# One of seven block products in the first adjacency product of a four-layer GNN is split into seven once more, and layer 0's node weights are loaded later

## The chip, the cores and the metric

The kernel runs on one core of one Trainium2 chip as a single launch. The metric is the device time of an execution in microseconds (us). Engine names are those of the profile: PE is TensorE's matmul and PEld its weight load, DVE is VectorE, ACT is ScalarE, POOL is GpSimd, SP is SyncE, which here only issues DMAs.

## The reference

`x` is 8 batches x 2048 nodes x 64 features, `adj` is a dense 2048 x 2048 matrix, and all is float32. Four layers follow each other, each `x = layernorm(x + f(x))`:

```
layer 0: f = sum over k of (A_k x) w_k(node) + bias(node)
         A_0 = I, A_1 = adj, A_2 = 2 adj adj - I
         w_k(node) = sum over d of embedding[node, d] * weight[d, k]     (d = 16)
layer 1: twice  z = relu(adj z W_i)
layer 2: x W_self + adj x W_neigh + bias
layer 3: [x, adj x, 2 adj adj x - x, and the last two again] W + bias
```

So the kernel has seven products of `adj` with a 2048 x 512 matrix (8 batches x 64 features side by side). The first of them, `adj x`, is the one that the change touches; the second, `adj (adj x)`, also belongs to layer 0 and uses the node weights.

## The kernel before

**Products by seven.** Each product except the first is cut by Winograd's form of Strassen's scheme: `adj` and the right factor are cut into 2 x 2 blocks, and seven block products of sums of blocks replace eight. The function `product` does this twice: its seven outer products are named A11, S1, A12, S2, S4, S3, A22, in this order, and the helper `inner` cuts each of them again into seven (the calls `mul`, four 128x512 matmuls each in layer 0). The sums of `adj`'s blocks that all later products need are made once, during the first product, and written to DRAM in the tensors `comb`.

**The first product, by slices.** `adj` arrives in four row slices of 512 rows, each in four chunks of 1 MB (`slice_chunk`, L157, on SP's queue, into a ring of four buffers). Slice 0 is computed plainly (`plain_slice`, L792). Slices 1 to 3 (`fast_slice`) use one level of the seven products: each is 16 matmuls 128x256 (`mul`, L829), 8 for each half of the columns. `raw(I, J)` is a block of the slice itself, `summed(S1)` and the like are sums of blocks that DVE makes in `prepare` (L643), tiles `si` and `so`. POOL's queue writes these to `comb` (L655). `T[0]` to `T[3]` are the four sums of blocks of x, so that `t_of(4)` stands for the fourth. The product of the slice's last quarter with it is `pd = mul(bank(), raw(1, 1), t_of(4))`, at L856; DVE later adds it to `p1` as `u3` (L851).

A slice's result `hT` is stored to DRAM (`keep_t1`, L771, SP's queue) and turned back into node order by `back`: four transposes on PE (L457) into a PSUM tile `pt` of the pool `p_tn`, which has two banks, and a copy by ACT (L458). A list of such jobs, `pump`, is served by one step after each half of a `mul`.

**Node weights of layer 0.** The tile `wn` holds weight[:, k] for three k, on both halves of the partitions. `load_weights`, after slice 0, loads it by two DMAs of 768 KB on SP's queue (L592), ahead of the small weights. In slice 2, `sum_wn` combines the three parts on DVE and subtracts the mean over the output features (`center`, L585 and L586). `wn` is first read by the matmuls of `feature0` (L970), in the second product.

**From the first product into the second.** The pools of the first product are closed and their memory is given to the pool `l0y`: `e_sb` (the embedding, loaded on POOL's queue, L938), `xT`, `tT` and `s`. `fetch` (L952) loads `xT` from the input and `tT` from the stored first product, on SP's queue. The `a` tiles of the second product come one for each `mul` from `blocks` (L203) or `comb` (L205), 1 MB each, in the ring of four, also on SP's queue. `product` takes an argument `between`, a function that is called after the outer products A11 and S1; the second product had none.

**Order.** A scheduler sets the order of the instructions on each engine and queue from the data dependencies; only instructions under `tc.keep_in_program_order` keep the order of the code among themselves. Each engine and each queue then runs in that order.

Of the kernel before, what the change touches and what calls it, by code (L numbers as in the profile page):

```python
# [9 lines left out]
F32 = mybir.dt.float32  # L10
AF = mybir.ActivationFunctionType
ALU = mybir.AluOpType
# [4 lines left out]
P = 128  # L17
EPS = 1e-5
GW = 512
TG = GW // P  # L20
# [83 lines left out]
def kernel(  # L104
# [358 lines left out]
    class Norm:  # L463
# [111 lines left out]


    if True:
        l0 = first.enter_context(tc.tile_pool(name="l0", bufs=1))

        wn = l0.tile([P, 3, D, F], F32, tag="wn", name="wn")  # L580

        def center(w, half=slice(0, P), pin=lambda inst: inst):
            shape = list(w.shape)
            m = small.tile([P, shape[1]], F32, tag="wm", name="wm")[half]
# [3 lines left out]
            ))  # L588

        def load_weights():  # L590
            for k in range(2):
                nc.sync.dma_start(wn[k * F : (k + 1) * F], w_l0.rearrange("n i d o -> i n d o"))  # L592
            nc.gpsimd.memset(wd, 0.0)
            w3 = sums.tile([P, 5, F], F32, tag="t", name="w3", bufs=5)
            for k in range(2):
                half = slice(k * F, (k + 1) * F)
                for i, src in ((W1A, w_l1[0]), (W1B, w_l1[1]), (W2N, w_neigh), (W2S, w_self)):
                    nc.sync.dma_start(wd[half, i, half], src)
                nc.scalar.dma_start(w3[half], w_l3.rearrange("(k i) o -> i k o", i=F))
            nc.sync.dma_start(b2, b_l2.to_broadcast([P, F]))  # L600
            nc.sync.dma_start(b3, b_l3.to_broadcast([P, F]))
            return w3

        def sum_wn():
            pin = tc.keep_in_program_order
            pin(nc.vector.tensor_tensor(wn[:, 0], wn[:, 0], wn[:, 2], ALU.subtract))
            pin(nc.vector.tensor_scalar(wn[:, 2], wn[:, 2], 2.0, None, ALU.mult))
            center(wn.rearrange("p n d o -> p (n d) o"), pin=pin)

        def sum_weights(w3):  # L610
            pin = tc.keep_in_program_order
# [26 lines left out]
        def prepare(ns, ch, outers):  # L638

            ch = [c.rearrange("p m i n -> p i m n") for c in ch]  # L640

            def add(out, a, b, op=ALU.add):
                inst = nc.vector.tensor_tensor(out, a, b, op)  # L643
                if ns:

                    tc.keep_in_program_order(inst)

            def kept(tag, shape, bufs):
                s = sums.tile([P, *shape, GW], F32, tag=tag, name="s" + ("i" if tag == "C" else "o"), bufs=bufs)
                n = "ab"[: len(shape)]  # L650
                return s, s.rearrange(f"p {' '.join(n)} (m n) -> p {' '.join(n)} m n", m=TG)

            def keep(q, s0, src):
                dst = comb[q][s0 : s0 + src.shape[1]].rearrange("s p (n c) -> p s n c", n=TG)
                nc.gpsimd.dma_start(dst[:, :, ns], src)  # L655

            def inner(q, q00, q01, q10, q11):
                flat, s = kept("C", (4,), 4)
                add(s[:, 0], q10, q11)
                add(s[:, 1], s[:, 0], q00, ALU.subtract)  # L660
                add(s[:, 2], q00, q10, ALU.subtract)
                add(s[:, 3], q01, s[:, 1], ALU.subtract)
                keep(q, 4, flat)

            def raw(I, J):
# [12 lines left out]
            def sq(s):  # L678
                return lambda c: s[:, :, c].rearrange("p a (m n) -> p a m n", m=TG)

            def put(q, s):
                flat = s.rearrange("p a b c -> p (a b) c")
                keep(q, 0, flat[:, :2])
                keep(q, 3, flat[:, 3:])
                inner(q, *(flat[:, k].rearrange("p (m n) -> p m n", m=TG) for k in range(4)))


            inner(A12, *raw(0, 1))
            inner(A22, *raw(1, 1))
# [12 lines left out]
            put(S4, s4)  # L702
            yield

        with tc.tile_pool(name="p_n", bufs=4, space=PSUM) as p_n, tc.tile_pool(
# [61 lines left out]
            def bank():  # L767
                return p_n.tile([P, GW], F32, tag="mm", name="ps_n")
# [7 lines left out]
            def new_h():  # L776
                return sums.tile([P, GW], F32, tag="t", name="hT", bufs=5)

            def back(ns, p, hT):
                to_nodes(1, p_tn, slice(ns, NT, TG), p, hT)  # L780
                yield
# [25 lines left out]
            def fast_slice(ns, ch, held):  # L807
# [5 lines left out]
                def raw(I, J):  # L813
                    return lambda j, m: ch[2 * J + j][:, m, 2 * I : 2 * I + 2]
# [7 lines left out]
                def t_of(n):  # L822
                    return lambda k, p: T[n - 1][:, k // 2, k % 2, ts(p, 2 * F)]

                def mul(ps, a, b, start=True):

                    for p in range(2):
                        for k in range(NT // 2):
                            nc.tensor.matmul(  # L829
                                ps[:, ts(p, GW // 2)], b(k, p), a(k // TG, k % TG),  # L830
                                start=(start and p == k == 0), stop=(k == NT // 2 - 1),
                                skip_group_check=True,
                            )
                        pump.step()
                    return ps
# [13 lines left out]
                def plus(tag, a, b):  # L849
                    u = sums.tile([P, GW], F32, tag=tag, name=tag)  # L850
                    nc.vector.tensor_tensor(u, a, b, ALU.add)  # L851
                    return u

                next(parts)
                p2 = mul(bank(), raw(0, 1), x_of(1, 0))
                pd = mul(bank(), raw(1, 1), t_of(4))  # L856
                load_chunks(ns + 1, 2, 3)
                for job in held:
                    pump.add(back(*job))
# [1 line left out]
                pa = mul(bank(), raw(0, 0), x_of(0, 0))  # L861
                p1 = sums.tile([P, GW], F32, tag="p1", name="p1")
                nc.scalar.copy(p1, pa)
                q3 = plus("u3", pd, p1)
                done(0, p2, p1)
                if ns == TG - 1:
                    join_bias(0, 1)
# [3 lines left out]
                load_chunks(ns + 1, 0, 1)  # L871
                if ns == 1:
                    sum_weights(w3)
                elif ns == 2:
                    sum_wn()
                else:
                    join_bias(0, 0)
                pb_ = mul(bank(), summed(S2), t_of(2))
                u2 = plus("u2", pb_, p1)
# [13 lines left out]
            for ns in range(TG):  # L893
                ch = [chunks.pop((ns, j)) for j in range(NG)]
                if ns == 0:
                    for n, _ in enumerate(prepare(ns, ch, {})):
                        if n == 1:
                            sums_of_x()
                    hT = plain_slice(ns, ch)
                    w3 = load_weights()  # L900
                    load_chunks(1, *AHEAD)
                    pump.add(biases())
                else:
                    hT = fast_slice(ns, ch, held)
                for p in range(NP):
                    keep_t1(ns, p, hT[p])

                held = []
                for p in range(NP):
                    if ns == TG - 2:  # L910
                        held.append((ns, p, hT[p]))
                    else:
                        pump.add(back(ns, p, hT[p]))
# [20 lines left out]
        if True:  # L934
            p_y = first.enter_context(tc.tile_pool(name="p_y", bufs=3, space=PSUM))
            l0y = first.enter_context(tc.tile_pool(name="l0y", bufs=1))
            e_sb = l0y.tile([P, NT, D], F32, tag="e_sb", name="e_sb")
            nc.gpsimd.dma_start(e_sb, emb)  # L938


            order = [
# [51 lines left out]


            RUNS = {S2: NP, S3: NP}
            product(1, then(feature0, 0, gap=4, pool_sq=True), rate=4, runs=RUNS)


    late = p_z = None
# [127 lines left out]
```

## Time and profile before

| what | value |
|---|---|
| median of 3 runs | 1670.58 us (1670.14 to 1670.74) |
| profiled execution | 1670.91 us, span of its instructions 1669.1 us |
| granted TensorE clock | 1.00 throughout |
| PE busy | 1660.6 us of 1669.1 |
| DVE, ACT, POOL busy | 945.8, 265.3, 246.0 us |
| slice 0 of the first product | PE from 5.7 to 61.0 us |
| slices 1, 2, 3 | PE from 61.0, 113.65, 163.75 to 213.9 us |
| second product begins | 216.2 us |
| first matmul with `wn` | about 312 us |

All times in the text count from the start of the span. A matmul of float32 stands in the trace as two records, so "x16" in a row of 128x256 matmuls is eight instructions; the time from the start of one record to that of the next is its pace, which is shorter than its duration since they overlap. The profile's bracket `[0.34 <-ACT xy L458]` says how long the engine stood idle before a row and what ended that. In rows of queues (SPq, POOLq) the time is that of issuing; the landing of a transfer is given apart.

### The profile page before, as it was taken

The page shows a single profiled execution, that of the slowest core. Times are in us where ns is not written, and L with a number is a line of the kernel's source. Part 1 is how long each engine was busy: PE and PEld are TensorE (multiplying, and loading weights), DVE is VectorE, ACT ScalarE, POOL GpSimd, SP SyncE. Part 2 cuts the span into 40 slices and gives each one's busy share as a digit, 9 for nine tenths or more (in the row PEclk, how much of TensorE's full clock was granted, in tenths as well). Part 3 has the DMA queues.
Part 4 walks back from the last instruction along what each step waited for, and adds up shares of the span by engine and source line. Part 5 has one row for each costly group of instructions (what it writes and reads, how often), then busy time and mean ns, then how long its engine had stood idle before and what let it go on. Part 6 is the DMA issues. An engine that isn't in the chain of part 4 may idle for free.

```text
span 1669.1 us, 20686 instructions
## 1 busy us (share of the span) xinstructions
PE 1660.6 (99%) x8182; PEld 1046.5 (63%) x8182; DVE 945.8 (57%) x1695; ACT 265.3 (16%) x766; POOL 246.0 (15%) x332
## 2 busy tenths in 40 slices
PE   9999999999999999999999999999999999999998
PEld 4688854444444444444454455589998455579998
DVE  6497884556456456654434365873568344443657
ACT  0100000142143044430010011220001011100001
POOL 1121200254155056650000000000000000000000
PEclk9999999999999999999999999999999999999999
DMA  9898898504603700019877877667888866678884
GB/s 352 331 373 310 302 334 307 189 27 147 227 26 108 271 26 26 26 51 369 286 264 272 308 263 253 229 225 260 297 297 295 306 212 232 229 267 292 316 308 171
DMA packets 82431, 391.52 MB, mean 235 GB/s; under 512 B 8896, under 2 KB 25536, under 8 KB 42784
## 3 DMA queue, kind: packets, MB, share of 16 engines
q1 hardware_dynamic: 69520, 346.78, 58.8%
q0 software_dynamic: 11248, 42.08, 6.6%
q10 hardware_dynamic: 1568, 1.35, 0.3%
q8 instruction: 65, 1.06, 0.3%
q14 instruction: 30, 0.25, 0.0%
HBM read 339.85 MB, written 50.33 MB: 234 GB/s over the span
## 4 chain that ended last, share of the span: by engine, by line
PE 98%; DMA 1%; DVE 0%; ACT 0%; issue 0%; ACTq 0%; DVEq 0%
PE y L970 20%; PE mmb L272 17%; PE mma L272 12%; PE mmc L272 12%; PE mmb L265 9%; PE ps_n L829 8%; PE mma L265 6%; PE mmc L265 6%; PE ps_n L792 3%; PE z L1022 3%; PE z L1051 2%; DMA a<-in_slices 1%; PE pt L1013 1%; DMA xy<-in_x 0%; PE pt_n L457 0%; PE mmd L265 0%
## 5 line engine op out<-in xcount | busy, mean ns | idle before, releaser
L272 PE MATMUL mmb<-a,t 128*128 128x512 f32 x648 | 292.0, 593 | 0.0
L980 DVE SCALAR_TENSOR_TENSOR xy<-y,e_sb,xy 128x128 f32<-128x128 f32 x512 | 179.6, 351 | 141.2 <-PE y L970 125.3
L272 PEld LDWEIGHTS mmb<-a,t 128*128 128x128 f32 x648 | 121.5, 190 | 145.3 <-issue 143.5
L989 POOL TENSOR_TENSOR s<-s 128x512 f32<-128x512 f32 (+2 forms) x192 | 157.1, 818 | 333.4 <-ACT s L984 323.2
L984 ACT ACTIVATE s<-y,e_sb 128x128 f32<-128x128 f32 x512 | 139.0, 382 | 231.8 <-PE y L970 231.8
L223 DVE TENSOR_TENSOR u<-mmb,p 128x512 f32<-128x512 f32 x84 | 57.8, 689 | 181.8 <-PE mmb L272 126.0
L265 PE MATMUL mmb<-t,a 128*128 128x128 f32 x1344 | 156.9, 275 | 0.0
L265 PEld LDWEIGHTS mmb<-t,a 128*128 128x128 f32 x1344 | 153.4, 192 | 0.0
L970 PE MATMUL y<-wn,xT 64*128 64x512 f32 x512 | 131.5, 590 | 0.0
L970 PE MATMUL y<-wn,tT 64*128 64x512 f32 x512 | 131.2, 589 | 0.0
L970 PE MATMUL y<-wn,C 64*128 64x512 f32 x512 | 131.2, 589 | 0.0
L272 PE MATMUL mma<-a,T 128*128 128x512 f32 x256 | 115.5, 594 | 0.0
L272 PE MATMUL mmc<-a,t 128*128 128x512 f32 x216 | 97.3, 592 | 0.0
L287 ACT COPY p<-mma 128x512 f32<-128x512 f32 x42 | 24.6, 586 | 404.4 <-PE mma L272 262.9
L970 PEld LDWEIGHTS y<-wn,xT 64*128 64x128 f32 x512 | 49.3, 187 | 61.2 <-issue 60.7
L970 PEld LDWEIGHTS y<-wn,tT 64*128 64x128 f32 x512 | 49.6, 187 | 60.3 <-issue 60.3
L970 PEld LDWEIGHTS y<-wn,C 64*128 64x128 f32 x512 | 49.6, 187 | 60.3 <-issue 60.3
L272 PE MATMUL mma<-a,xy 128*128 128x512 f32 x192 | 86.7, 593 | 0.0
L272 PEld LDWEIGHTS mma<-a,T 128*128 128x128 f32 x256 | 47.6, 190 | 56.8 <-issue 56.5
L223 DVE TENSOR_TENSOR C<-mmc,C 128x512 f32<-128x512 f32 x48 | 33.2, 692 | 85.9 <-PE mmc L272 75.1
L272 PEld LDWEIGHTS mmc<-a,t 128*128 128x128 f32 x216 | 40.0, 190 | 45.4 <-issue 45.2
L829 PE MATMUL ps_n<-a,xy 128*128 128x256 f32 x288 | 64.7, 380 | 0.1
(140 smaller groups left out, 2047.2 us busy)
## 6 DMA issues: line engine op xcount, KB each, us to landing
a<-comb SPq DMA_DIRECT2D x240, 1024.0 KB, 4.8
a<-in_blocks SPq DMA_DIRECT2D x54, 1024.0 KB, 4.8
comb<-si POOLq DMA_DIRECT2D x28, 1024.0 KB, 10.5
a<-in_slices SPq DMA_DIRECT2D x15, 1024.0 KB, 9.4
comb<-so POOLq DMA_DIRECT2D x16, 512.0 KB, 6.7
comb<-so POOLq DMA_DIRECT2D x16, 256.0 KB, 8.4
t1T<-hT SPq DMA_DIRECT2D x16, 256.0 KB, 4.2
xT<-in_xT SPq DMA_DIRECT2D x16, 256.0 KB, 3.4
```

The source lines that it names most:

```text
L223: nc.vector.tensor_tensor(out, a, b, op)
L265: nc.tensor.matmul(to, a[:, k, m, :], xb[:, m, :], start=(start and opens and m == 0), stop=(m == TG - 1), skip_group_check=True,)
L272: nc.tensor.matmul(ps, xb[:, m, :], a[:, :, m, :], start=(start and m == 0), stop=(m == TG - 1), skip_group_check=True,)
L287: nc.scalar.copy(p1, pa)
L792: mm = nc.tensor.matmul(ps[p], xcol(0, TG * j + m, p), ch[j][:, m], start=(n == 0 and m == 0), stop=(n == NG - 1 and m == TG - 1), skip_gr ...
L829: nc.tensor.matmul(ps[:, ts(p, GW // 2)], b(k, p), a(k // TG, k % TG), start=(start and p == k == 0), stop=(k == NT // 2 - 1), skip_group_ ...
L970: mm = nc.tensor.matmul(y[:, b, :], terms[n][half, ts(k, P)], wn[half, n, h * DH : (h + 1) * DH, :], start=(n == 0), stop=(n == 2),)
L980: nc.vector.scalar_tensor_tensor(acc, y[:, :, ts(d, F)], e, acc, ALU.mult, ALU.add)
L984: nc.scalar.activation(s[:, d], y[:, :, ts(d, F)], AF.Copy, scale=e)
L989: nc.gpsimd.tensor_tensor(s[:, :n], s[:, :n], s[:, n : 2 * n], ALU.add)
L1022: nc.tensor.matmul(z[:, k, :], aT[:, ts(k, P)], wd[:, w, :], start=(n == 0), stop=(n == len(terms) - 1),)
L1051: nc.tensor.matmul(z[n][:, k], xT[half, ts(k, P)], w[half], start=True, stop=True)
```

## The change

1. In slices 1 to 3, the product `raw(1, 1)` times `t_of(4)` is no longer 16 matmuls 128x256 but a second level of seven products (`two_level`), each four matmuls 128x128: 28 matmuls. They go in turn to two banks of the pool `p_tn`, that of the transposes, and ACT copies each result out before the bank is used again. DVE joins the parts by two additions and adds `p1`.
2. The sums of `adj` that the second level needs are the `si` tile of A22 that DVE made already; it is now made ahead of that of A12. The sums of x, tile `t4`, are made once in slice 0 by four more DVE additions 128x512 (`sums_t`).
3. The pool `l0` is gone. `wn` is now a tile of `l0y`, in memory of the first product, and its two DMAs of 768 KB are on POOL's queue, after `e_sb`. `sum_wn` is the `between` of the second product, and centers the three parts one by one.

```diff
-        wn = l0.tile([P, 3, D, F], F32, tag="wn", name="wn")
...
         def load_weights():
-            for k in range(2):
-                nc.sync.dma_start(wn[k * F : (k + 1) * F], w_l0.rearrange("n i d o -> i n d o"))
...
+            outers[A22] = inner(A22, *raw(1, 1))
             inner(A12, *raw(0, 1))
-            inner(A22, *raw(1, 1))
...
+            def sums_t(b, t):
+                b11, b12, b21, b22 = b
+                for n, (x, y) in enumerate(((b12, b11), (b22, t[0]), (b22, b12), (b21, t[1]))):
+                    nc.vector.tensor_tensor(t[n], x, y, ALU.subtract)
+
+            b4 = [T[3][:, 2 * j : 2 * j + 2, :, ts(p, 2 * F)] for j in range(2) for p in range(2)]
+            t4 = xs.tile([P, 4, TG, 2 * F], F32, tag="t4", name="t4")
+            t4 = [by_tiles(t4[:, n]) for n in range(4)]
+            turn = [0]
+
+            def two_level(raw, sums_, b, t, out):
+                banks = [p_tn.tile([P, TG, P], F32, tag="pt", name="ps_i")[:, 0] for _ in range(2)]
+                pa, pb_ = banks[:: 1 - 2 * (turn[0] % 2)]
+                turn[0] += 1
...
+                part = xs.tile([P, 3, P], F32, tag="part", name="part", bufs=2)
+
+                def mul(ps, n, x, start, to):
+                    for m in range(TG):
+                        nc.tensor.matmul(
+                            ps, x[:, m // 2, m % 2], s[n](m), start=(start and m == 0),
+                            stop=(m == TG - 1), skip_group_check=True,
+                        )
+                    nc.scalar.copy(to, ps)
+
+                mul(pa, 0, b11, True, part[:, 0])
+                mul(pb_, 5, t2, True, part[:, 1])
+                mul(pa, 1, b21, False, out[:, 0, 0])
+                mul(pb_, 6, t3, False, part[:, 2])
+                mul(pa, 4, t1, True, out[:, 1, 1])
+                mul(pb_, 3, t4, False, out[:, 0, 1])
+                mul(pa, 7, b22, False, out[:, 1, 0])
+                o = out.rearrange("p a b n -> p (a b) n")
+                nc.vector.tensor_tensor(
+                    o[:, 1:], o[:, 1:], part[:, 0].unsqueeze(1).to_broadcast([P, 3, P]), ALU.add
+                )
+                nc.vector.tensor_tensor(o[:, 2:], o[:, 2:], part[:, 1:], ALU.add)
...
                 p2 = mul(bank(), raw(0, 1), x_of(1, 0))
-                pd = mul(bank(), raw(1, 1), t_of(4))
+                q3 = new_out("u3")
+                two_level(
+                    lambda i, j: lambda m: ch[2 + j][:, m, 2 + i], outers[A22], b4, t4, by_blocks(q3)
+                )
                 load_chunks(ns + 1, 2, 3)
...
-                q3 = plus("u3", pd, p1)
+                nc.vector.tensor_tensor(q3, q3, p1, ALU.add)
...
-                elif ns == 2:
-                    sum_wn()
-                else:
+                elif ns == TG - 1:
                     join_bias(0, 0)
...
             nc.gpsimd.dma_start(e_sb, emb)
+            wn = l0y.tile([P, 3, D, F], F32, tag="wn", name="wn")
+            for k in range(2):
+                nc.gpsimd.dma_start(wn[k * F : (k + 1) * F], w_l0.rearrange("n i d o -> i n d o"))
+
+            def sum_wn():
+                pin = tc.keep_in_program_order
+                pin(nc.vector.tensor_tensor(wn[:, 0], wn[:, 0], wn[:, 2], ALU.subtract))
+                pin(nc.vector.tensor_scalar(wn[:, 2], wn[:, 2], 2.0, None, ALU.mult))
+                for n in range(3):
+                    center(wn[:, n], pin=pin)
...
-            product(1, then(feature0, 0, gap=4, pool_sq=True), rate=4, runs=RUNS)
+            product(1, then(feature0, 0, gap=4, pool_sq=True), sum_wn, rate=4, runs=RUNS)
```

More of the change, by code (lines that the diff above doesn't have):

```diff
@@ L577 @@
     if True:
-        l0 = first.enter_context(tc.tile_pool(name="l0", bufs=1))
-        wn = l0.tile([P, 3, D, F], F32, tag="wn", name="wn")
         def center(w, half=slice(0, P), pin=lambda inst: inst):
@@ L602, in load_weights @@
             return w3
[L604 to L608, printed above, removed]
         def sum_weights(w3):
@@ L663, in inner @@
                 keep(q, 4, flat)
+                return flat
             def raw(I, J):
@@ L777, in new_h, with by_tiles @@
                 return sums.tile([P, GW], F32, tag="t", name="hT", bufs=5)
+            def by_tiles(v):
+                return v.rearrange("p (a b) c -> p a b c", b=2)
+            def sums_t(b, t):
[3 more added lines that the diff above has]
+            b4 = [T[3][:, 2 * j : 2 * j + 2, :, ts(p, 2 * F)] for j in range(2) for p in range(2)]
@@ new lines @@
+            t4 = xs.tile([P, 4, TG, 2 * F], F32, tag="t4", name="t4")
[5 more added lines that the diff above has]
+                turn[0] += 1
+                b11, b12, b21, b22 = b
+                t1, t2, t3, t4 = t
+                s = [raw(i, j) for i in range(2) for j in range(2)]
+                s += [lambda m, n=n: sums_[:, n, ts(m, P)] for n in range(4)]
+                part = xs.tile([P, 3, P], F32, tag="part", name="part", bufs=2)
[18 more added lines that the diff above has]
+                nc.vector.tensor_tensor(o[:, 2:], o[:, 2:], part[:, 1:], ALU.add)
@@ L779, in back, with new_out, by_blocks @@
+            def new_out(tag):
+                return sums.tile([P, GW], F32, tag=tag, name=tag)
+            def by_blocks(v):
+                return v.rearrange("p (a b n) -> p a b n", a=2, b=2)
             def back(ns, p, hT):
@@ L895 @@
                 if ns == 0:
-                    for n, _ in enumerate(prepare(ns, ch, {})):
+                    outers = {}
+                    for n, _ in enumerate(prepare(ns, ch, outers)):
                         if n == 1:
                             sums_of_x()
+                            sums_t(b4, t4)
                     hT = plain_slice(ns, ch)
```

## The prediction

> **What bounds the kernel now.** I read the page first (busy shares, then the chain that ended last), then PE's timeline over the first product, the chain over the same stretch, and the issues of SP's queue where the second product begins. Busy shares and chain, from the page:
>
> ```profile
> PE 1660.6 (99%) x8182; PEld 1046.5 (63%) x8182; DVE 945.8 (57%) x1695; ACT 265.3 (16%) x766; POOL 246.0 (15%) x332
> ...
> PE 98%; DMA 1%; DVE 0%; ACT 0%; issue 0%; ACTq 0%; DVEq 0%
> ```
>
> PE is idle for 8.5 us in all and is 98% of the chain. So PE time that is taken away is gained, and a wait of PE that is added is lost, unless it falls into one of those few gaps. The price of a matmul is its pace. PE's timeline: first three rows of 128x256 records in the slices, then two of 128x128 records with the same 128x128 weights in a later product (start, duration, records).
>
> ```profile
> 78.29 4.00 PE L829 MATMUL ps_n<-a,xy 128*128 128x256 f32 x16
> ...
> 136.13 13.98 PE L829 MATMUL ps_n<-so,T 128*128 128x256 f32 x64
> 149.94 13.98 PE L829 MATMUL ps_n<-so,xy 128*128 128x256 f32 x64
> ...
> 1102.58 3.74 PE L265 MATMUL mmb<-t,a 128*128 128x128 f32 x32
> 1106.15 3.74 PE L265 MATMUL mma<-xy,a 128*128 128x128 f32 x32
> ```
>
> Start to start, 64 records of 256 columns take 13.81 us, 215.8 ns each; 32 of 128 columns take 3.57 us, 111.6 ns each. The first row is 0.38 us longer than its like (3.62). The chain of waits over the first 330 us shows why:
>
> ```profile
> 61.23 19.03 DMA a<-in_slices
> 80.30 1.99 PE ps_n L829 x8
> ```
>
> Slice 1's last chunk of adj is issued at 61.23 and lands at 80.26; PE waits for it. Elsewhere in the slices PE has no gap. The second place is the start of the second product. SP's issues there, and PE's row that reads the last of them:
>
> ```profile
> 214.51 2.65 SPq L771 DMA_DIRECT2D t1T<-hT  x4
> 219.23 1.11 SPq L952 DMA_DIRECT2D tT<-t1T  x2
> 220.43 0.38 SPq L205 DMA_DIRECT2D a<-comb  x1
> ...
> 230.32 3.60 PE L272 MATMUL mmc<-a,C 128*128 128x512 f32 x8
> ```
>
> SP stores slice 3's result, waits until that has landed, loads it back (tT), and only then issues the `a` tile of the fifth inner product. It lands 7.7 us later, at 228.15; PE begins its weights at 229.89. **1.7 us is all the margin there.** Two of the windows of 5 us around it (busy times by engine, clock, DMA share, GB/s) show the DMA engines full:
>
> ```profile
> 210.00:215.00 5.00, 4.92 (x26) 4.04 (x25) 1.12 (x4) 0.00 (x0) 0.00 (x0) 1.00 1.00 406
> 215.00:220.00 5.00, 4.66 (x18) 2.48 (x19) 4.96 (x7) 2.25 (x4) 0.00 (x0) 1.00 1.08 378
> ```
>
> **What the skill says.** (a) The Trainium skill, "DMA: Bandwidth & Descriptors", section "Issuing engines are not separate DMA queues": DMAs of all issuing engines end on the same 16 DMA engines and interleave. The trace agrees: between 210 and 220 us SP's queue holds 54% of them and POOL's 50%, at 392 GB/s together. Moving `wn` to POOL's queue therefore gives it no bandwidth of its own. (b) "TensorE: Matmul & The Clock Gate", section "LDWEIGHTS (loading the stationary operand)": 128 columns of weights take P/1.2, 107 ns. A 128-column record needs one such load, and the trace's pace of 111.6 ns lies just above it; halving the columns gives 52% of the time, not less. (c) "ScalarE: Activation LUTs", section "What ACT_TABLE_LOAD costs": 186 ns + 0.833 ns an element without pointer operands. That makes 613 ns for 512 elements, against 586 measured (L458), so I take 293 ns for ACT's new 128x128 copies, an estimate.
>
> **The change, part by part.**
>
> *1. The product itself.* Removed in each of three slices: 16 matmuls, 32 records x 215.8 ns = 6.91 us. Added: 28 matmuls, 56 records x 111.6 = 6.25 us. Gain 0.66 us a slice, 1.97 in all. An eighth of the multiplications is saved, and of that the weight loads leave three quarters.
>
> *2. Turns between the two banks.* Each group of four matmuls takes 0.893 us, and its bank is written again one group later. Transposes show the turnaround: the copy by ACT starts 0.04 us after the last record's end and PE goes on 0.06 us after the copy. From the next group's start: 0.16 (the last record's overlap) + 0.04 + 0.29 + 0.06 = 0.56 us, below 0.893, and below 0.65 too, when PE would like to begin the weights. Cost 0; what hides it is the group on the other bank. The transposes before share the banks, but the reversed order on every second slice puts the bank used last second. If the estimate is too low by up to 0.3 us, five or six turns in three slices lose up to 0.2 us each, so 0 to 3 us; below nothing is excluded, since no wait is taken away here.
>
> *3. DVE in the slices.* Added per slice: two joins (by columns at 685 ns per 512, 0.5 and 0.4 us), and four sums of x once (2.7 us). DVE waits 6.9 us in slice 0 for a write to `comb`, and 7.3 in slice 2 and 6.0 in slice 3 for `p1`; these cover them. The first sums of A22 are made 2.4 us earlier than now, in slice 2 by 118 us against 121 us when PE needs them. `sum_wn` leaves slice 2, 8.6 us of DVE that PE did not wait for. Cost and gain 0.
>
> *4. The chunk of slice 1.* PE arrives 0.66 us earlier at a transfer that lands at 80.26. If it lands as now, slice 1 gains nothing. If it lands over 1 us earlier, the 0.38 us wait goes as well: gain 1.04. For earlier: `wn` (1.57 MB, about 4 us at 392 GB/s) leaves the queue ahead of it. Against: `wn` had landed by 37 us, and the issue at 61.23 follows PE's last use of the buffer, which does not move. I take half, 0.5, with 0 and 1.04 as ends. Slices 2 and 3 give 1.31.
>
> *5. The load of `wn`, moved.* In the order that the scheduler gives POOL, the first half stands after `e_sb` (200.5 us now, released by PE's last use of the closed pool), then two writes of sums to `comb` (205.1 and 207.6), then the second half. All of 1.57 MB is put on DMA engines that are full from 208 on: 3.8 to 4.0 us of work. The stores of slice 3 (512-byte rows) come behind or between, so tT is issued later, and behind it on SP the `a` tile of the fifth inner product. Delay of that tile: 4 us, less what fits in holes between 200 and 206 (about 1 us). Minus the margin of 1.7 us: **a new wait of PE of about 1.3 us**, ends 0 and 2.2. The next tiles have margins of 3 and 4 us and, being delayed no further, cost nothing more. The two `comb` writes behind the first half are not read before the outer products S4 and S3, over 60 us on.
>
> *6. `sum_wn` in the second product.* Now 1.22 + 0.69 + 3.35 + 3.35 us; in three parts 1.22 + 0.69 + 3 x (1.2 + 1.2) = 9.1 us, an estimate from the same rows. In DVE's order it is spread between S1's last addition (264.9 us) and A12's evictions. Added up in that order, `u` is ready at 273.0 with its bank wanted at 274.95, the next at 276.7 against 278.4, the third at 280.3 against 281.8. Margins of 1.5 us or more: cost 0. Its input landed some 40 us earlier.
>
> **Sum:** -1.31 - 0.5 + 0 + 1.3 = -0.5 us against the profiled execution's 1670.91, so 1670.4; the median of the runs lies 0.33 below that execution, so **1670.1 us**. After 290 us the order on every engine is the same as before.
>
> **Rivals.**
>
> *A. The new DMA wait takes most of the gain (the forecast).* For: the full DMA engines and the margin of 1.7 us. Against: the stretch's first 6 us aren't full. -1.3 to +0.9 us, by the ends of the wait: 1669.3 to 1671.5. Chance 0.52.
>
> *B. No new wait.* The delayed stores shift by less than 1.7 us because the second half of `wn` finds holes. Then -1.8 us, with the whole of part 4 -2.35: 1668.8 to 1668.2. Chance 0.33. To pass 0.2% (3.3 us) it would also need a gain that I can't name; I give that 0.08 of the 0.33.
>
> *C. The turns between the banks decide, and it is slower.* If a turn takes longer than 0.893 us, PE waits at every one of 15 turns. Against a gain of 1.8 us it becomes slower from 0.12 us a turn, that is from a turnaround of 1.01 us; with the DMA wait from 0.03 us. It passes 0.2% with 0.26 us a turn, 1.15 us in all. Against: a copy four times as wide turned in 0.85. With 0.26 us a turn and the DMA wait the result is 1674. Chance of C 0.15, about half of it beyond 0.2%.
>
> That the change doesn't do what it says is no rival: PE's order in the changed program shows the 28 matmuls in three slices.
>
> **How the numbers follow.** About 0.2% is what a measurement of this kernel can tell from no change; that is 3.3 us, from 1667.2 to 1673.9, and both likely cases lie inside. Faster by more: 0.08. Within: 0.85 (A 0.52, B 0.25, half of C 0.08). Slower: 0.07. The range takes B's best, 1668.2, and A with slice 1's gain lost and the wait at its upper end, +0.9 and some tenths of C: 1671.9.
>
> **What would show each step.** Right: 56 records of `ps_i` in about 6.25 us without a gap, a wait of PE on a DMA of `a` at the fifth inner product near 228 us, no wait of PE on DVE near 265 to 280. Wrong: gaps on ACT between groups of `ps_i` (part 2); no wait near 228 and a second product that begins and goes on 2 us earlier (part 5); the chunk of slice 1 landing at 80.3 again (part 4); PE waiting for `u` on DVE (part 6). A result outside 1668 to 1672 would mean a cost or gain that is not in this list.

## The result, and the profile after

The changed kernel takes **1676.39 us** (median of 6 runs, 1675.31 to 1677.32) against 1670.61 for the kernel before (6 runs on the same chip, 1670.14 to 1670.91): a ratio of 1.0035, with a 95% interval of 1.0022 to 1.0047. It is 5.8 us slower. The forecast was 1670.1, between 1668.2 and 1671.9. The profiled execution took 1676.53 us, 0.14 above the median (before: 0.30 above); its span is 1674.6.

Busy shares and the chain of the page, after:

```profile
PE 1661.0 (99%) x8254; PEld 1049.6 (63%) x8254; DVE 951.6 (57%) x1709; ACT 270.5 (16%) x787; POOL 246.8 (15%) x334
...
PE 98%; DMA 1%; DVE 0%; issue 0%; SPq 0%; DVEq 0%
```

PE is still the bound, and its busy time has grown by 0.4 us although multiplications were taken away. Two places explain all of it. The first is what was meant. PE's timeline in slice 1 (start, duration, records) begins and ends the second level so:

```profile
70.42 1.06 PE L798 MATMUL ps_i<-a,xy 128*128 128x128 f32 x8
...
75.82 1.06 PE L798 MATMUL ps_i<-si,xy 128*128 128x128 f32 x8
76.72 3.62 PE L873 MATMUL ps_n<-a,xy 128*128 128x256 f32 x16
```

From 70.42 to 76.72 the 56 records take 6.30 us, without a gap; slices 2 and 3 take 6.30 and 6.25. The row after them, which had waited 0.38 us for a chunk, no longer waits: the chunk lands at 75.98 us. The second product begins at 213.80 us; it began at 216.15. **Up to there the change has gained 2.35 us**: 1.88 in the three products, 0.38 at the chunk, and 0.09 that was there already at the start of slice 1 (60.95 us instead of 61.04).

The second place is the fifth inner product of A11. PE's timeline there:

```profile
213.80 1.02 PE L272 MATMUL mma<-a,xy 128*128 128x512 f32 x2
...
224.54 3.60 PE L272 MATMUL mmb<-a,C 128*128 128x512 f32 x8
233.82 5.85 PE L272 MATMUL mmc<-a,C 128*128 128x512 f32 x8 [5.68 <-DMA a<-comb]
239.51 3.60 PE L272 MATMUL mmb<-a,C 128*128 128x512 f32 x8
```

Two things stand in the third row. In brackets: PE was idle for **5.68 us** until the `a` tile had landed. And the eight records took 5.85 us instead of 3.60; from this start to the next are 5.69 us, where the pace gives 3.43, so **some 2.3 us more**. Four windows of 2 us (busy times by engine, then granted clock, DMA share, GB/s) show why:

```profile
230.00:232.00 2.00, 0.00 (x0) 0.00 (x0) 2.00 (x3) 0.00 (x0) 0.00 (x0) 0.85 0.97 398
232.00:234.00 2.00, 0.18 (x1) 0.21 (x2) 1.87 (x1) 0.00 (x0) 0.00 (x0) 0.50 1.06 446
...
236.00:238.00 2.00, 2.00 (x3) 0.67 (x2) 0.00 (x0) 0.00 (x0) 0.00 (x0) 0.50 1.06 446
238.00:240.00 2.00, 2.00 (x6) 0.83 (x5) 0.29 (x1) 0.00 (x0) 0.00 (x0) 0.94 0.82 348
```

The clock falls to half at about 231.4 us, 3.3 us after PE became idle at 228.14, and is back at about 238.2. The sum -2.35 + 5.68 + 2.3 = +5.6 us is the difference between the two profiled executions (1676.53 - 1670.91 = 5.62). So nothing else of size has to be looked for.

Why the tile came late stands in the rows of SP's queue:

```profile
212.17 8.10 SPq L760 DMA_DIRECT2D t1T<-hT  x4
225.06 0.81 SPq L1010 DMA_DIRECT2D tT<-t1T  x2
225.96 0.38 SPq L205 DMA_DIRECT2D a<-comb  x1
```

The four stores of `t1T` take SP 8.10 us to issue instead of 2.65, and the first lands at 224.99, 12.8 us after its issue (4.7 before). tT waits for it, and the `a` tile stands behind tT: issued at 225.96 and landed at 233.68, though PE came for it at about 228. The second half of `wn` landed at 224.79, just ahead of that first store. The windows of 5 us, with the last number the GB/s moved:

```profile
205.00:210.00 5.00, 5.00 (x24) 4.40 (x24) 2.84 (x3) 0.00 (x0) 1.37 (x2) 1.00 1.01 267
210.00:215.00 5.00, 4.58 (x26) 3.21 (x25) 3.28 (x5) 1.66 (x3) 0.00 (x0) 1.00 1.00 340
```

The DMA engines are full (share 1.01 and 1.00) and yet move only 267 and 340 GB/s; before, the same two windows had 388 and 406. **Full engines with fewer bytes: the load of `wn` costs more than its bytes.** That became the last question of the study.

### The profile page after: what moved, and what is told of

It reads as the page before. It is cut to its first block, busy times and chain, and to the rows that moved or that the text cites. A ratio compares the mean times of both kernels' runs of the same rounds, so it can differ in the third digit from the quotient of the medians.

```text
span 1674.6 us, 20882 instructions
## 1 busy us (share of the span) xinstructions
PE 1661.0 (99%) x8254; PEld 1049.6 (63%) x8254; DVE 951.6 (57%) x1709; ACT 270.5 (16%) x787; POOL 246.8 (15%) x334
## 3 DMA queue, kind: packets, MB, share of 16 engines
q10 hardware_dynamic: 1568, 1.35, 0.3%
q8 instruction: 66, 1.08, 0.3%
## 4 chain that ended last, share of the span: by engine, by line
PE 98%; DMA 1%; DVE 0%; issue 0%; SPq 0%; DVEq 0%
PE y L1028 20%; PE mmb L272 17%; PE mmc L272 12%; PE mma L272 11%; PE mmb L265 9%; PE ps_n L873 7%; PE mma L265 6%; PE mmc L265 6%; PE ps_n L836 3%; PE z L1080 3%; PE z L1109 2%; PE ps_i L798 1%; PE pt L1071 1%; DMA t1T<-hT 1%; DMA a<-comb 0%; PE pt_n L457 0%
## 5 line engine op out<-in xcount | busy, mean ns | idle before, releaser
L1080 PEld LDWEIGHTS z<-wd,C 128*128 128x128 f32 x384 | 50.2, 192 | 21.7 <-issue 20.7
```

The costliest lines, as they stand in the source:

```text
L1080: nc.tensor.matmul(z[:, k, :], aT[:, ts(k, P)], wd[:, w, :], start=(n == 0), stop=(n == len(terms) - 1),)
```

## The experiments

Theory L: the whole loss is the load of `wn` at the end of the first product, which delays the stores of `t1T`, through them tT, and on SP's queue the `a` tile; the half clock follows from PE's idle time. Rival P: the product by seven, or the sums that moved with it, costs something of its own. Rivals within L: SP's order against plain bandwidth, and the size of the load. Each kernel was timed beside the kernel before, on the same chip; the median of the kernel before was 1670.5 to 1670.7 us each time.

Slice 1 begins between 60.4 and 61.4 us in the twelve traces. To compare executions that start a little apart, the table counts from the second product's first matmul. PE comes to the fifth inner product 14.2 us after it if nothing holds it up, and loads the weights, the `a` tile, 0.4 us earlier.

| kernel | median, us | ratio to before (95% interval) | `a` tile lands after, us | wait of PE, us |
|---|---|---|---|---|
| before | 1670.6 | | 12.0 | 0 |
| changed | 1676.39 | 1.0035 (1.0022 to 1.0047) | 19.9 | 5.68 |
| no load | 1668.40 | 0.9988 (0.9981 to 0.9995) | 12.1 | 0 |
| move only | 1678.21 | 1.0048 (1.0031 to 1.0065) | 19.8 | 5.59 |
| tT on POOL's queue | 1670.14 | 0.9998 (0.9989 to 1.0007) | 15.1 | 0.86 |
| load late | 1668.56 | 0.9989 (0.9982 to 0.9995) | 12.2 | 0 |
| second half late | 1672.04 | 1.0009 (1.0002 to 1.0016) | 16.2 | 1.94 |
| two queues | 1676.50 | 1.0036 (1.0023 to 1.0049) | 20.4 | 6.23 |
| six pieces | 1675.06 | 1.0030 (1.0019 to 1.0042) | 19.0 | 4.76 |
| all partitions | 1672.13 | 1.0008 (0.9999 to 1.0017) | 16.0 | 1.84 |
| four matmuls more | 1674.32 | 1.0027 (1.0017 to 1.0036) | 19.6 | 1.89 |
| two matmuls more | 1675.82 | 1.0032 (1.0020 to 1.0045) | 19.9 | 3.91 |

Three of these kernels have a wait of about 1.9 us in their profiled execution (second half late, all partitions, four matmuls more). Part of their runs (12 of 20, 8 of 12 and 4 of 10) are longer, most of them by about 2 us, and list a mean clock of 0.997 or 0.998 instead of 0.999 or 1.000, which lifts the medians. In those the clock seems to have fallen; no trace of one was taken, and the part on the half clock comes back to it.

### No load, and the move alone

```diff
-            for k in range(2):
-                nc.gpsimd.dma_start(wn[k * F : (k + 1) * F], w_l0.rearrange("n i d o -> i n d o"))
+            nc.gpsimd.memset(wn, 0.01)
```

> The changed kernel with one thing left out: the two transfers of wn. POOL fills the tile with a constant instead, so the node features of layer 0 are not those of the reference; every other instruction stays. Theory L (the whole loss comes from the load at the end of the first product): the second product begins at 213.8 us as in the changed kernel, the stores of t1T land 4 to 5 us after their issue (12.8 in the changed kernel), the wait of 5.68 us before the fifth inner product is 0 to 0.6 us, the granted clock stays 1.00, and the time is 1670.6 - 2.35 = 1668.2 us, up to 1668.8. Theory P (the product by seven, its sums on DVE or the weight sums in the second product cost something that the trace hides): some 1670 us or more, with a wait that is still there without the load.

Measured: 1668.40 us. The second product begins at 213.53, the stores of `t1T` land 5.4 to 5.6 us after their issue (a little over the expected 4 to 5), and the fifth product follows without a wait; the clock is 1.00 in every window from 205 to 275 us. SP's queue and the row of PE:

```profile
211.90 2.60 SPq L760 DMA_DIRECT2D t1T<-hT  x4
217.33 1.05 SPq L1009 DMA_DIRECT2D tT<-t1T  x2
218.47 0.38 SPq L205 DMA_DIRECT2D a<-comb  x1
```

```profile
227.71 3.60 PE L272 MATMUL mmc<-a,C 128*128 128x512 f32 x8
```

The second experiment is the other half, the kernel before with only the load and `sum_wn` moved:

```diff
-        wn = l0.tile([P, 3, D, F], F32, tag="wn", name="wn")
...
+            wn = l0y.tile([P, 3, D, F], F32, tag="wn", name="wn")
+            for k in range(2):
+                nc.gpsimd.dma_start(wn[k * F : (k + 1) * F], w_l0.rearrange("n i d o -> i n d o"))
```

> The kernel before, with the moved load of wn and its moved sums alone; the fourth quarter stays one plain product. Theory L: the second product begins at 216.15 us as before, the load makes the a tile of the fifth inner product land at about 233.7 us as in the changed kernel, where it is needed at 229.9: a wait of 3.8 us, and if that idle time also halves the clock another 2.4 us: 1674.4 us without and 1676.8 us with the clock. Theory P: the load costs nothing by itself, 1670.6 us.

Measured: 1678.21 us, above both numbers. PE's timeline:

```profile
226.83 3.60 PE L272 MATMUL mmb<-a,C 128*128 128x512 f32 x8
236.02 5.17 PE L272 MATMUL mmc<-a,C 128*128 128x512 f32 x8 [5.59 <-DMA a<-comb]
```

The wait is 5.59 us, not 3.8. My expectation had kept the landing time of the changed kernel, 233.7 us, but POOL's second half of `wn` follows the last writes to `comb`, and those follow the slice: everything behind it moves with the end of the first product (landing at 235.89). This kernel also shows where the 0.38 us at the chunk of slice 1 come from: here, too, the chunk lands early, at 77.10 us, and PE's row, at 78.62, takes 3.62 us and has no wait, though the product is the plain one. So that gain belongs to the load, which is no longer ahead of the small weights, and not to the product by seven. In the trace 5.59 + 1.6 for the half clock - 0.4 at the chunk is 6.8 us; the profiled executions differ by 7.04 and the medians by 7.56.

So theory L holds and P falls. The kernel without the load is 2.3 us faster than the one before (1668.40), of which, by the traces, 1.9 are the product by seven and 0.4 the chunk. The moved load costs 7.6 us alone, with the 0.4 already taken off; 7.6 - 1.9 is 5.7, and the result was 5.8.

### SP's order, or bandwidth

Here only the first two loads of tT leave SP's queue for POOL's:

```diff
-                        nc.sync.dma_start(tile_, src[p][:, ts(i, GW)])
+                        queue = nc.gpsimd if src is t1T and k < 2 else nc.sync
+                        queue.dma_start(tile_, src[p][:, ts(i, GW)])
```

> The changed kernel with the first two loads of tT on POOL's queue, behind wn, so that SP's queue does not wait for the stores of t1T before it issues the a tiles; the same bytes are moved in the same stretch. Theory Q (the loss is SP's order: the a tile was issued at 226 us because tT stood ahead of it): the a tile is issued at 215 to 219 us, lands before 228, the wait is 0 to 0.5 us, 1668.2 to 1668.8 us. Theory B (the loss is bandwidth: the 16 DMA engines are busy from 198 to 235 us, and the same bytes need the same time whatever their order): the eighth a tile still lands near 240 us where it is needed at 237.9, the waits of PE come to 2 to 4 us in smaller pieces, each too short for the clock to fall: 1670.5 to 1672.5 us.

Measured: 1670.14 us, 1.7 above the kernel without the load: between the two theories. SP's queue and PE:

```profile
212.62 7.83 SPq L760 DMA_DIRECT2D t1T<-hT  x4
220.54 0.72 SPq L205 DMA_DIRECT2D a<-comb  x1
```

```profile
229.46 3.67 PE L272 MATMUL mmc<-a,C 128*128 128x512 f32 x8 [0.86 <-DMA a<-comb]
```

The stores still land at 225.08, 12.5 us after their issue, but nothing on SP waits for them now. The tile is issued at 220.54 instead of 225.96, and the wait shrinks from 5.68 to 0.86 us, too little for the half clock. **So most of the loss is the wait in SP's order behind tT, and only the rest can be bandwidth.** The 7.83 us of the first row show what remains: SP is still held up while it issues the stores. The later tiles came some 0.1 us late each (the fifth and sixth products take 3.5 us from start to start); the two to four microseconds that theory B saw there did not come. The wait and these come to 1.0 of the 1.7 us; in the two traces the other 0.7 lies in the start of slice 1, at 61.40 instead of 60.67 us.

### The load later

Each half now waits for a result of the second product, by a one-column copy on ACT:

```diff
+                for k, late in enumerate((u[:, 1], v[:, 0])):
+                    half = slice(k * F, (k + 1) * F)
+                    nc.scalar.copy(wn[half, 0, 0, :1], late[half, :1])
+                    nc.gpsimd.dma_start(wn[half], w_l0.rearrange("n i d o -> i n d o"))
+                sum_wn()
```

> The changed kernel with the two halves of wn loaded later: ACT writes one column of each half from a result of the second product (the seventh inner product of A11, the third of S1), and POOL's transfer of that half follows it, so the halves start near 238 and 248 us; the order on PE, DVE and SP is that of the changed kernel. Theory L: the stores of t1T and the a tile of the fifth inner product come as in a kernel without the load, and the 1.5 MB go into the gaps of the DMA engines between 238 and 271 us (share 0.75 to 0.93 there), where four a tiles are on the way at a time: 1668.2 to 1668.8 us. Rival: the load costs the same wherever it lies beside the a tiles, since each half slows them by some 4 us and two tiles on the way have only about 1.4 us of margin each: waits of 2 to 5 us, 1670.5 to 1673 us.

Measured: 1668.56 us, a ratio of 0.9989 (0.9982 to 0.9995). **This version beats both kernels**, by 2.1 and by 7.8 us, with a complete load. The halves were issued at 240.00 and 249.30 and landed at 247.02 and 259.44. Two of the windows there:

```profile
240.00:245.00 5.00, 5.00 (x14) 2.13 (x12) 5.00 (x4) 0.59 (x1) 0.64 (x1) 1.00 1.01 303
...
255.00:260.00 5.00, 5.00 (x13) 2.15 (x12) 2.58 (x4) 0.00 (x0) 0.00 (x0) 1.00 1.02 284
```

PE is busy for all 5.00 us, though the load fills the DMA engines just as before; the `a` tiles land 6.5 to 9.4 us after their issue instead of 4.8, and PE does not wait for one of them. Here each tile is issued a whole ring ahead and stands behind nothing that must land first. In these windows, too, full engines move only 284 to 303 GB/s.

### Half of the load

The first half stays where the change put it, and only the second comes later:

```diff
+            load_wn(0)
...
+                k = 1
+                nc.scalar.copy(wn[k * F : (k + 1) * F, 0, 0, :1], u[:, 1][k * F : (k + 1) * F, :1])
+                load_wn(k)
```

> The changed kernel with the first half of wn where the change put it and only the second half later (after ACT's copy of one column from the seventh inner product of A11, near 238 us). Theory L in proportion to the bytes: both halves together delay the a tile of the fifth inner product by 5.6 us of wait and 1.74 us of margin, 7.3 us; one half delays it by 3.7 us, of which the margin takes 1.74: a wait of 1.9 us, too short for the clock to fall, and 1668.5 + 1.9 = 1670.4 us. Rival, all of it from the second half (issued last, still on the way when the stores of t1T are issued): no wait, 1668.5 us. Rival, all of it from the first half: a wait of 5.6 us and the half clock as in the changed kernel, 1676.4 us.

Measured in the trace: a wait of 1.94 us, where 1.9 was expected.

```profile
230.56 3.67 PE L272 MATMUL mmc<-a,C 128*128 128x512 f32 x8 [1.94 <-DMA a<-comb]
```

The tile lands 4.0 us later than without the load, with both halves 7.8 us later: the delay goes with the bytes, and neither half alone is to blame. The profiled execution took 1671.02 us (expected: 1670.4). The median is 1672.04, and the runs spread from 1669.7 to 1674.8, as told at the table.

### The half clock by itself

Matmuls whose result is overwritten fill a part of the wait, four in one kernel (shown) and two, `range(2)`, in the other:

```diff
             pc = bank("c")
+            if src == 1 and home is not None:
+                for m in range(4):
+                    tc.keep_in_program_order(nc.tensor.matmul(
+                        pc, b11[:, m % TG, :], xy[:, 0, src, :], start=True, stop=True,
+                        skip_group_check=True,
+                    ))
             mul(pc, 4, t1, True)
```

> The changed kernel with four matmuls more on PE (8 records, 3.43 us) between the fourth and the fifth inner product of A11, into the accumulator that the fifth then overwrites, with operands that are there: work without use, in a stretch in which PE waits anyway. The a tile lands when it did. Theory C (the 2.42 us after the wait come from PE's idle time): 5.68 us of idle time become 2.25 us, the clock stays 1.00, the fifth product takes 3.43 us again: 1676.4 - 2.4 = 1674.0 us. Rival (the clock falls for another reason, such as the load on the DMA engines): 1676.4 us, the eight records after the wait still at 5.85 us.

> As the last, with two matmuls (4 records, 1.72 us): 3.96 us of idle time are left. If idle time of that length already halves the clock, 1676 to 1676.4 us, with a clock under 1.00 in the stretch from 230 to 240 us; if it takes longer than that, 1674.0 us and 1.00.

Measured: 1674.32 us with four matmuls, 1675.82 with two. The row of PE after the wait and the window from 235 us, first with four:

```profile
233.77 3.70 PE L272 MATMUL mmc<-a,C 128*128 128x512 f32 x8 [1.89 <-DMA a<-comb]
...
235.00:240.00 5.00, 5.00 (x13) 2.21 (x12) 5.00 (x4) 0.00 (x0) 0.00 (x0) 1.00 1.00 424
```

and with two:

```profile
234.10 5.40 PE L272 MATMUL mmc<-a,C 128*128 128x512 f32 x8 [3.91 <-DMA a<-comb]
...
235.00:240.00 5.00, 5.00 (x9) 2.09 (x8) 0.47 (x1) 0.00 (x0) 0.00 (x0) 0.66 0.99 418
```

The tile lands at the same time in both (233.7 and 234.1), and DMA is as busy. Useless work ahead of the wait makes the kernel 2.1 us faster, since the eight records then run at full clock. So the half clock comes from PE's idle time: 3.91 us of it brought it on, and 1.89 did not in the profiled execution.

The length alone doesn't say when. In the kernel with the move alone PE was idle from 230.43 to 236.02 us, and the windows there are:

```profile
230.00:235.00 5.00, 0.43 (x2) 0.00 (x0) 4.67 (x5) 0.00 (x0) 0.00 (x0) 1.00 0.91 312
235.00:240.00 5.00, 3.98 (x6) 1.89 (x7) 1.16 (x1) 0.00 (x0) 0.00 (x0) 0.66 1.00 423
```

The clock was still whole at 235 us. The trace's record of the clock has the fall at 235.64, 5.2 us after PE became idle, where the changed kernel took 3.3.

The clock records of all the traces show when it can change. Each stretch at one clock, apart from the last, which the end of the kernel cuts off, lasts a whole number of steps of 3.413 us: one or two at half clock (3.41 or 6.83 us), 66 or 67 from the clock's first rise to its fall (225.28 or 228.69 us). So it changes only at marks 3.41 us apart, and these lie otherwise in each execution. What fits all the traces is the idle time between two neighbouring marks. With two matmuls more, the 3.91 us lay across a mark: 1.85 us came before it, and the clock stayed; 2.06 came after it, and at the next mark the clock fell, although PE had been at work again for 1.35 us. In the three traces with a wait of about 1.9 us, the most between two marks was 1.64, 1.79 and 1.84 us, and the clock stayed. These waits are close to that border, so a small shift could decide in the longer runs of those kernels; no trace shows it.

The marks also give the size of the loss. In the changed kernel PE works at half clock from 233.82 us to the mark at 238.22, and half of these 4.4 us are 2.2 of the 2.3 us.

The Trainium skill, "TensorE: Matmul & The Clock Gate", section "What's actually happening", gives an idle window of about 3.4 us after which the clock is halved, and calls it free-running. The marks agree with that. But the window need not be idle throughout: here one with 2.06 us of idle time was enough, and the measurement decides.

### The size of the load

1.57 MB at the 424 GB/s of the `a` tiles alone would be 3.7 us; the tile was delayed by 7.8. The trace's packet records show where the rest is. Without `wn` beside it an 8,192-byte packet of `a` took 309 ns; from 208 to 212 us in the changed kernel it took 477 (medians), and the 4,096-byte packets of `wn` 231. With tT beside it, in the kernel with tT on POOL's queue, `a` stayed at 309 and the 4,096-byte packets took 159. The difference that I saw was that each half of `wn` goes to 64 partitions. The first try put the halves on two queues:

```diff
-                nc.gpsimd.dma_start(wn[k * F : (k + 1) * F], w_l0.rearrange("n i d o -> i n d o"))
+                (nc.gpsimd, nc.scalar)[k].dma_start(
+                    wn[k * F : (k + 1) * F], w_l0.rearrange("n i d o -> i n d o")
+                )
```

> The changed kernel with the second half of wn on ACT's queue instead of POOL's, so that the two halves are on the way at the same time; bytes, tiles and the order on PE, DVE and SP stay. Theory H (the load was mis-sized because each half of wn is written to 64 partitions only, which by the Trainium skill's page SBUF - State Buffer, Door 1, reach 8 of the 16 ports: partitions 0 to 63 one set, 64 to 127 the other; in the run that loads wn late its 4,096-byte packets took 328 ns, where those of tT, which go to all 128 partitions, took 159 ns beside the same a tiles): two halves at a time use all ports, the packets go back toward 159 ns, 1.57 MB cost 3.7 us at 424 GB/s and not 7.3, the wait before the fifth inner product is 3.7 - 1.74 = 2.0 us, the clock stays 1.00, and the time is 1668.5 + 2.0 = 1670.5 us. Rival (two streams of reads slow each other, whatever the partitions): three streams at once, packets still at 250 to 330 ns, the same wait of 5 to 6 us with the half clock, some 1676 us.

Measured: 1676.50 us and a wait of 6.23. The packets of `wn` still took 238 ns and those of `a` 481, and the window shows it:

```profile
205.00:210.00 5.00, 5.00 (x25) 4.41 (x24) 3.30 (x4) 0.00 (x0) 0.75 (x1) 1.00 1.00 273
```

As it was put, the theory failed: two halves at a time are no quicker. The Trainium skill, "SBUF — State Buffer", section "Can I just issue two DMAs to hit both halves?", says the same, which my expectation had not taken in: two transfers, one to each half, gave only 6% over one. The six pieces gave as little:

```diff
+            for n in range(3):
+                for k in range(2):
+                    nc.gpsimd.dma_start(wn[k * F : (k + 1) * F, n], w_l0[n])
```

> The changed kernel with the load of wn cut into six transfers of 256 KB, partitions 0 to 63 and 64 to 127 in turn, all still on POOL's queue. Theory H, if pieces of one queue overlap on the 16 engines: between 1670.5 and 1676 us, with packets shorter than in the changed kernel. Theory H, if the engines work through one queue in step: the pieces follow each other, each on half of the ports, and the time is that of the changed kernel, 1676.4 us. The rival of the last run: 1676.4 us too.

Measured: 1675.06 us, a wait of 4.76, the packets at 228 and 465 ns. What is left of the theory is the form of each single transfer, and that has a direct test, in which the rows loaded are not those that layer 0 needs:

```diff
+            rows = w_l0.rearrange("n i d o -> (n i) d o")
+            for n in range(3):
+                nc.gpsimd.dma_start(wn[:, n], rows[n * F // 2 : n * F // 2 + P])
```

> The changed kernel with wn loaded in three transfers of 512 KB that each go to all 128 partitions: the same 1.57 MB from the same weights in 4,096-byte rows, but rows 32 n to 32 n + 127 of the flattened weights instead of the right ones, so the node features of layer 0 are not those of the reference. Theory H (64 partitions a transfer are what slows the load, and two transfers at a time, as in the run with two queues, still collide): packets of wn at 159 ns and of a at 309 ns where the two run together, 3.7 us of work and not 7.3, a wait of 2.0 us before the fifth inner product, no half clock, 1670.5 us. Rival (the partitions don't matter; the source, or two streams of reads, slows both): 4,096-byte packets at 210 to 330 ns and those of a at 450 to 670 ns as in the changed kernel, a wait of 5 to 6 us, 1675 to 1676.5 us.

Measured in the trace, PE's row and the same window:

```profile
229.64 3.67 PE L272 MATMUL mmc<-a,C 128*128 128x512 f32 x8 [1.84 <-DMA a<-comb]
...
205.00:210.00 5.00, 5.00 (x25) 4.41 (x24) 2.49 (x2) 0.00 (x0) 0.69 (x1) 1.00 1.00 416
```

416 GB/s instead of 267 or 273. From 204 to 208 us the packets of `wn` take 159 ns and those of `a` 309, side by side. The tile is delayed by 3.9 us instead of 7.8, and the wait is 1.84 us (expected: 2.0). The profiled execution takes 1670.14 us (expected: 1670.5); the median is 1672.13, since eight of the twelve runs are among the longer ones told of at the table. All three transfers are issued early here, by 199.73 us, where the changed kernel issued its second half at 206.03; but with two queues both halves were issued by 199.49 and nothing was gained, so it isn't that. Nor is it the cut into pieces: six of them made up for only 0.9 us of the delay. So **the same bytes cost twice as much when each transfer goes to 64 partitions, and they slow the `a` tiles beside them as well.** The Trainium skill, "SBUF — State Buffer", section "Door 1: The DMA port swizzle", says that partitions 0 to 63 reach 8 of the 16 ports, some 218 GB/s: 7.2 us for 1.57 MB, an estimate from that figure, beside the 7.8 measured. In the kernel with the late load no packet of `a` starts from 243 to 245 us, and those of `wn` take 328 to 339 ns (medians of each us): 16 engines with 4,096 bytes in that time are some 200 GB/s, an estimate from the trace, and at 159 ns they are 412. How the ports hold up the transfers of the neighbours wasn't measured.

## Why the prediction was wrong

1. *The product itself:* right. 6.25 to 6.30 us for 56 records, as worked out.
2. *Turns between the banks:* right, 0. No row of `ps_i` has a wait, and rival C is excluded. (The terms given add up to 0.55 and not 0.56, which changes nothing.)
3. *DVE in the slices:* right, 0. PE waits for nothing there.
4. *The chunk of slice 1:* I took 0.5 us, a guess halfway between 0 and 1.04; the upper end came. The chunk lands 4.3 us earlier. The reason "for" was the right one, since the chunk came early in the kernel with the move alone, too.
5. *The load of `wn`:* **this step failed**, not in its mechanism but in its size. Stores, tT, SP's order, the `a` tile and the fifth inner product are where the text put them. But "3.8 to 4.0 us of DMA work" came from all of its bytes at 392 GB/s, and the transfers of 64 partitions needed 7.8. With transfers of 128 partitions the same load delays the tile by 3.9 us, so the term would have been right for those. The hole of "about 1 us" didn't show either: 3.9 - 1.7 of margin would be 2.2 us, the upper end that I gave, and 1.84 to 1.94 us were measured for a delay of that length. The margin was somewhat larger than 1.7, which I had counted to the start of the weights: the matmuls begin 0.14 us after the tile has landed (233.68 and 233.82), so it is needed 14.0 us after the product's first matmul, and it had landed at 12.0.
6. *`sum_wn` in the second product:* right, 0. PE has no wait between 255 and 330 us.

What was missing altogether is the price of idle time, a term put at nothing without a reason: I counted a wait of PE at its own length. At 5.68 us it also brought 2.3 us of half clock. "A result outside 1668 to 1672 would mean a cost or gain that is not in this list": it was this one, on top of the mis-sized load. With both in it, the sum would have been -2.35 + 5.68 + 2.3, or 5.6 us.

Of the rivals, B gave 1668.2 to 1668.8 for the case without a new wait. That is where the kernels without the load (1668.40) and with the late load (1668.56) landed: it had the gain right and the wait wrong. No rival gave the DMA more than +0.9 us; the slower end was given to the bank turns, which cost nothing. Rival A's ends, -1.3 to +0.9, also leave out the 0.5 of part 4 that the sum has; with it they are -1.8 to +0.4.

## What to carry to other kernels

When a transfer is moved into a stretch where the DMA engines are full, size it by its own rate there and not by its bytes at the rate of others: look up how long its packets take in the trace, and be wary of one that goes to half of the partitions. Then ask what lands behind it and what stands behind that on an in-order queue: here a wait of a load for a store, ahead of the tiles that PE lives on, turned a delay into idle time, and the same load 40 us later, beside tiles issued a ring ahead, cost nothing. And a wait of PE can cost more than its length: here those of 3.9 us and more did, and those of 1.9 did not in the traces taken.

## What the runs showed of the hardware that I had not expected

- Packets of 4,096 bytes to 64 partitions took 231 ns beside packets of `a`, and in the kernel with the late load 328 ns (242 to 246 us), against 159 ns to 128 partitions. The 8,192-byte packets of `a` beside them went from 309 to 477 ns, and to 673 in those 4 us of the late load, where only 20 of them started.
- Idle time of 3.91 to 6.23 us, in five kernels, lengthened the eight records after it by 1.6 to 2.8 us. Waits of about 1.9 us left them at full clock in three profiled executions. The clock changed only at marks 3.413 us apart, 3.3 to 5.3 us after PE had become idle, and an interval between two marks in which PE was idle for 2.06 us was enough, while 1.85 us were not.
- SP needed 8.10 us to issue four stores of 512-byte rows while the load of `wn` was on the way, and 2.60 to 2.65 without it. Full DMA engines alone don't explain it, since their share was 1.00 and 1.08 in the windows of the kernel before, too; the cause stays open.
